# Five score banks, one pool of four weight tiles and block transposes for every duo in a decoder layer on one core

## The chip, the core and the metric

The kernel runs on one core of one Trainium2 chip. A core has five engines that run side by side, each through its own list of instructions in order: TensorE (PE, matrix products; PEld is its loading of the stationary operand), VectorE (DVE), ScalarE (ACT), GpSimd (POOL) and SyncE (SP, which here only issues transfers). SBUF is the working memory of 128 partitions. PSUM receives the products; it has 8 banks, and a bank holds 512 float32 values in each partition. Transfers (DMAs) are issued from an engine's queue and carried out by 16 transfer engines. An instruction starts when the semaphores that it waits for have reached their values.

The metric is the device time of one execution in microseconds (us). The time before is 1978.22 us, the median of 3 runs (1977.18 to 1980.28).

## The reference

It is one decoder layer in float32 on x of shape 4 x 1024 x 256: self-attention, cross-attention to 64 context rows, and a feed-forward part that picks one of 64 small networks for each row. Each part is added to its input.

```python
x = x + attn(layernorm(x))     # 16 heads of 64, 4 key/value heads, all 1024 keys, no mask
x = x + xattn(layernorm(x))    # 16 heads of 16, 64 keys
x = x + ffn(layernorm(x))      # gelu and tanh to two numbers, choice of 1 of 64 splines, layernorm

# attn, for each batch, head and query row
scores = einsum('bqhd,bkhd->bhqk', q * scale, k)
probs = softmax(scores)
out = einsum('bhqk,bkhd->bqhd', probs, v)
```

Nearly all of the work is the self-attention: 4 batches x 16 heads x 1024 x 1024 scores.

## The kernel before

**Tiles.** A batch has 8 query tiles of 128 rows. A query tile has 8 head pairs (two heads z = 0, 1 that lie in the two halves of the partitions), so that there are 4 x 8 x 8 = 256 "rows" of work: one row is 128 queries of two heads against 1024 keys. Two rows (i = 0, 1) make a duo; there are 128 duos, 32 in each batch.

**One row** (function `duo`, lines 566 to 688). `scores` (L592) multiplies queries with keys: 4 products of 512 keys, two for each head, into a PSUM tile `s` of two banks per head. `largest` (L606, VectorE) takes the maximum of each head's 1024 scores. `exponential` (L612, ScalarE) writes the softmax weights, before division, into the tile `prob` and adds up their sum.

**The weights' transpose.** For the product with the values the weights must lie with the keys on the partitions. There are two ways to that. For three duos of four (`by_array(d)` false) VectorE transposes 32 x 32 blocks in place (`turn`, L621, one instruction of 128 x 1024 per head and row), and 16 transfers from SyncE's queue (`carry`, L648, 128 KB each) move the blocks from `prob` to their partitions in a second tile, `probT`. For the fourth (d % 4 == 3) TensorE transposes 128 x 128 tiles (`flips`, L631) into PSUM tiles of the pool `p1`, and ScalarE copies them out (L635).

**The product with the values** (`values`, L671) reads `probT` in two parts into a PSUM tile `av` with a bank of its own, and ScalarE copies it to `heads` (L686). `project` (L691) inverts the sums, spreads them over the partitions through DRAM (`rsT`, `rsD`, `rb`), divides on GpSimd (L710), and multiplies with the output weights (L728).

**Beside the rows** run the projections of queries, keys and values (L545, L494, L517), the layer norms (L403), the cross-attention (from L797) and the feed-forward part (from L1023), as tasks that fill the time between.

**PSUM.** `s` has 2 tiles of 2 banks, `p1` 3 banks, `av` 1: all 8. `prob` and `probT` have 2 places each.

**The order of work** is not that of the loops. Every step is handed to a planner, the class `Flow` (L78 to L189), by `add(engine, cost, key, emit, reads, writes, ...)`: its engine, an assumed cost in us, a due number, what it reads and writes. `order` then plays through time and always takes the task that can start first, score, maximum and exponential ("urgent") before others, and in this order the instructions are written into the engines' lists. A task's results count as ready for other engines after a lag (`LAG`, or a `lag` of its own for transfers). `places` says how many tiles of each name there are. `SLACK` keeps a task from being put just ahead of an urgent one that is about to be ready. What really runs waits on semaphores; a wrong cost only makes a poorer order.

Of the kernel before, what the change touches and what calls it, by code (L numbers as in the profile page):

```python
# [17 lines left out]
P = 128  # L18
# [38 lines left out]
class Buf:  # L57


    def __init__(self, tag=None, make=None, whole=None):  # L60
        self.tag, self.make, self.whole = tag, make, whole or self
        self.writers, self.readers, self.parts = [], [], {}
        self.uses, self.first, self.left, self.last, self.t = set(), None, 0, 0.0, None

# [13 lines left out]
class Flow:  # L78
# [7 lines left out]
    AHEAD, SLACK = 16, 0.4  # L86
    LAG = {"PE": 0.3, "DVE": 0.2, "ACT": 0.25, "POOL": 0.25}
# [5 lines left out]
    def add(self, engine, cost, key, emit, reads=(), writes=(), lag=None, holds=(), lead=False, urgent=False):  # L93
# [4 lines left out]
        for b in writes:  # L98
            t.need.update(b.readers)
        t.need.discard(t)  # L100
# [19 lines left out]
    def order(self):  # L120
        free = {tag: [0.0] * n for tag, n in self.places.items()}
# [14 lines left out]
        while todo:  # L136
            best = None
            for engine, some in could.items():
                pick = None
                soon = min((t.ready for t in some if t.urgent), default=inf)  # L140
                for t in some:
# [4 lines left out]
                    for b in t.takes:  # L146
# [4 lines left out]
                        start = max(start, free[b.tag][k])  # L151
                    else:
                        if not t.urgent and start < soon < start + t.cost - self.SLACK:
                            start = soon
# [10 lines left out]
            for b in t.takes:  # L165
                free[b.tag].pop(0)
                if b.tag in self.lines:
                    self.lines[b.tag].remove(b)
# [8 lines left out]
            for b in t.bufs:  # L177
                b.left -= 1
                b.last = max(b.last, t.end)
                if not b.left:  # L180
                    insort(free[b.tag], b.last + 0.2)
            yield t

    def emit(self):
        for t in self.order():
            for b in t.takes:
                b.t = b.make()
# [5 lines left out]
def decoder(  # L193
# [26 lines left out]
    ps_s = ctx.enter_context(tc.tile_pool(name="ps_s", bufs=2, space=PSUM))  # L220
    ps_1 = ctx.enter_context(tc.tile_pool(name="ps_1", bufs=3, space=PSUM))
    ps_o = ctx.enter_context(tc.tile_pool(name="ps_o", bufs=1, space=PSUM))
# [5 lines left out]
            s=2, p1=3, o=1, x=3, xn1=2, xT=1, kT0=1, kT1=1, vn=4, qT=12, prob=2, probT=2, sums=3, nmax=4,  # L228
# [8 lines left out]
    def buf(tag, pool, *shape, bufs=None, name=None):  # L237
        bufs = flow.places[tag] if bufs is None else bufs
        return Buf(tag, lambda: pool.tile([P, *shape], F32, tag=tag, name=name or tag, bufs=bufs))

    def psum1(name):

        return Buf("p1", lambda: ps_1.tile([P, 512], F32, tag="p1", name=name))
# [159 lines left out]
    def layernorm(key, name, src, dst, w, reads, writes):  # L403

        st = Buf("ln", lambda: (
            small.tile([P, w, 6], F32, tag="bnst", name=f"{name}_st", bufs=2),
            small.tile([P, w, 2], F32, tag="bnmv", name=f"{name}_mv", bufs=2),
            small.tile([P, w], F32, tag="bnrs", name=f"{name}_rs", bufs=2),
# [20 lines left out]
        add("DVE", 0.6 * w, key, stats, reads, [st], holds=writes)  # L429
        add("POOL", 1.0, key, rsqrt, [st], [st])  # L430
        add("ACT", 0.45 * w, key, apply, [st, *reads], writes)

    def transposed(key, name, src, dst, k, reads, write):
# [12 lines left out]
        add("PE", 0.55, key, flips, reads, [pt], holds=[write])  # L446
# [6 lines left out]
    halves = (slice(0, HD), slice(HD, P))  # L453
    xs, xTs, kTs, vns, qTs, sums, heads = {}, {}, {}, {}, {}, {}, {}

    def by_array(d):

        return d % 4 == 3
# [27 lines left out]
    def keys(b, j, key):  # L486

        kT = kTs[b, j] = buf(f"kT{j}", big, S, name=f"kT_{b}_{j}")
        for g in range(2):
# [15 lines left out]
            add("PE", 1.75, key, project, [wk_, xTs[b].part(2 * g), xTs[b].part(2 * g + 1)], [pk], holds=[kT])  # L505
            add("ACT", 0.7, key, evict, [pk, colv_], [kT])

    def value_rows(b, g, key):
# [24 lines left out]
        add("PE", 1.75, key, project, [wv_, xTs[b].part(g)], [pv], holds=[vn])  # L533
        add("DVE", 0.69, key, evict, [pv, rowv_], [vn])

    def queries(b, w, c, key):
# [16 lines left out]
        add("PE", 1.8, key, project, [wq_, xTs[b].part(w)], [pq], holds=[qTs[b, w, c], qTs[b, w, c + 1]])  # L553
# [12 lines left out]
    def duo(b, d):  # L566
# [7 lines left out]
        prob = Buf("prob", lambda: work.tile([P, 4 * S], F32, tag="prob", name=f"prob_{b}_{d}"))  # L574
        probT = Buf("probT", lambda: work.tile([P, 4 * S], F32, tag="probT", name=f"probT_{b}_{d}"))
# [7 lines left out]
        for i in range(2):  # L583
# [3 lines left out]
            ps = [Buf("s", lambda z=z: ps_s.tile([P, S], F32, tag="s", name=f"s_{b}_{d}_{i}_{z}")) for z in range(2)]  # L587

            def scores(ps=ps, q=q, kT=kT):
                for g in range(2):  # L590
                    for z, r in enumerate(halves):
                        mm(  # L592
                            ps[z].t[:, 512 * g : 512 * (g + 1)],
# [6 lines left out]
            add("PE", 1.95, n - 3, scores, [q, kT], ps, holds=[prob, ss], lead=True)  # L600
            for z in range(2):
                k = z * QC + c
                nmax = buf("nmax", small, 1, name=f"nmax_{b}_{d}_{i}_{z}")

                def largest(z=z, nmax=nmax, ps=ps):
                    nc.vector.tensor_reduce(nmax.t, ps[z].t, AX.X, ALU.max, negate=True)  # L606

                def exponential(z=z, i=i, k=k, nmax=nmax, ps=ps):
                    src = ps[z].t
# [6 lines left out]
                add("DVE", 1.22, n - 3, largest, [ps[z]], [nmax], urgent=True)  # L616
                add("ACT", 1.33, n - 3, exponential, [ps[z], nmax], [prob.part((z, i)), ss.part(k)], urgent=True)
                if not by_array(d):
# [4 lines left out]
                    add("DVE", 1.25, n - 1, turn, [prob.part((z, i))], [prob.part((z, i))])  # L623
                else:
                    for g in range(2):
# [11 lines left out]
                        add("PE", 0.54, n - 1, flips, [prob.part((z, i))], [pt], holds=[probT])  # L637
                        add("ACT", 0.6, n - 1, evict, [pt], [probT.part((z, g))])

        if not by_array(d):  # L640


            for k in range(4):
                for qb in range(4):
                    r = (qb + k) % 4

                    def carry(qb=qb, r=r):
                        nc.sync.dma_start(  # L648
# [654 lines left out]
```

## Time and profile before

| what | value |
|---|---|
| median of 3 runs | 1978.22 us |
| the profiled execution: its time | 1978.13 us |
| its span, first to last instruction | 1976.4 us |
| TensorE busy | 1737.7 us (88%) |
| VectorE busy | 1400.9 us (71%) |
| ScalarE busy | 1062.5 us (54%) |
| GpSimd busy | 554.1 us (28%) |
| mean granted TensorE clock | 0.939 of full speed |
| block transfers | 1536, all from SyncE's queue |

In the lines of the profile, "L606 DVE TENSOR_REDUCE nmax<-s 128x1 f32<-128x1024 f32 x512 | 601.9, 1216 | 342.7 <-PE s L592 341.4" reads: line 606, VectorE, the operation, output and input with shapes, 512 of them, 601.9 us busy in all, 1216 ns for one; the engine was idle for 342.7 us just before them, of which 341.4 ended when TensorE's scores of line 592 were done. Two instructions that follow each other closely overlap at their ends, so that the busy time of a group is less than its count times the duration of one. A float32 product is two instructions on TensorE. Semaphore and transfer-issuing instructions do not count as busy. In a timeline the columns are start, length, engine, line and operation, and in brackets the idle time before.

### The profile page before, as it was taken

The numbers are of one execution on the slowest core, as the hardware profiler recorded it, in microseconds if no ns is written. First come the engines' busy times: TensorE is split into PE (matmuls) and PEld (weight loads), VectorE is DVE, ScalarE is ACT, GpSimd is POOL, SyncE is SP. The second block draws the span as 40 slices with busy tenths as digits, with TensorE's granted clock in tenths as the row PEclk, the third lists the DMA queues.
The fourth block names the chain that finished last, engine by engine and source line by source line (L and its number), as shares of the span: only waits on it lengthen the run. The fifth ranks groups of instructions, "written<-read, shape, count | busy, mean of one in ns | idle before, by whom it ended". The sixth has DMA issues, their size and how long they took to land.

```text
span 1976.4 us, 28894 instructions
## 1 busy us (share of the span) xinstructions
PE 1737.7 (88%) x10180; PEld 1025.7 (52%) x10180; DVE 1400.9 (71%) x2036; ACT 1062.5 (54%) x1977; POOL 554.1 (28%) x872
## 2 busy tenths in 40 slices
PE   6898989889998998989999898988999899997842
PEld 4455555555654555555655454555555455554521
DVE  4667777886778766787677676787677876778632
ACT  3445556656564655655565555655565455555511
POOL 1001213152122512225031522316122350304352
PEclk8889999999998999999999898999999899999965
DMA  3566455455655455566454456545555645445500
GB/s 131 128 139 150 115 140 122 115 146 125 138 129 136 106 137 124 121 152 150 102 134 107 123 136 139 139 116 126 136 116 116 157 118 129 105 111 130 139 23 12
DMA packets 95455, 243.05 MB, mean 123 GB/s; under 512 B 28368, under 2 KB 39376, under 8 KB 95312
## 3 DMA queue, kind: packets, MB, share of 16 engines
q1 hardware_dynamic: 91504, 229.39, 49.6%
q0 software_dynamic: 2704, 9.46, 1.7%
q10 hardware_dynamic: 1104, 2.37, 0.3%
q8 instruction: 81, 1.33, 0.3%
q14 instruction: 62, 0.51, 0.1%
HBM read 35.32 MB, written 4.46 MB: 20 GB/s over the span
## 4 chain that ended last, share of the span: by engine, by line
PE 64%; DVE 16%; ACT 6%; POOL 5%; DMA 3%; SPq 3%; issue 3%; POOLq 0%; DVEq 0%; ACTq 0%
PE s L592 22%; PE av L671 18%; DVE nmax L606 6%; PE pq L545 5%; PE po L728 4%; PE ptp L631 4%; DVE prob L621 3%; SPq L648 3%; ACT prob L612 3%; PE pk L494 1%; PE pv L517 1%; DMA par<-in_table,tile 1%; PE pxt L898 1%; PE xs L837 1%; PE pxq L814 1%
## 5 line engine op out<-in xcount | busy, mean ns | idle before, releaser
L606 DVE TENSOR_REDUCE nmax<-s 128x1 f32<-128x1024 f32 x512 | 601.9, 1216 | 342.7 <-PE s L592 341.4
L612 ACT ACTIVATE prob<-s,nmax 128x1024 f32<-128x1024 f32 x512 | 568.8, 1114 | 407.3 <-DVE nmax L606 388.7
L592 PE MATMUL s<-kT,qT 64*128 64x512 f32 x2048 | 584.4, 639 | 35.0 <-ACT prob L612 34.6
L671 PE MATMUL av<-probT,vn 128*64 128x256 f32 x4096 | 499.4, 396 | 29.5 <-DMA probT<-prob 26.0
L621 DVE STREAM_TRANSPOSE prob<-prob 128x1024 f32<-128x1024 f32 x384 | 458.6, 1223 | 37.7 <-ACT prob L612 26.8
L671 PEld LDWEIGHTS av<-probT,vn 128*64 128x64 f32 x4096 | 298.2, 142 | 252.3 <-issue 111.7
L592 PEld LDWEIGHTS s<-kT,qT 64*128 64x128 f32 x2048 | 212.9, 192 | 266.5 <-issue 163.6
L710 POOL TENSOR_TENSOR heads<-heads,rb 128x256 f32<-128x256 f32 x128 | 90.0, 729 | 607.6 <-DMA rb<-rsD 503.7
L635 ACT COPY probT<-ptp 128x512 f32<-128x512 f32 x256 | 137.8, 590 | 74.3 <-PE ptp L631 72.5
L631 PE MATMUL ptp<-ident,prob 128*128 128x128 f32 x1024 | 141.1, 281 | 34.0 <-ACT prob L612 30.4
L631 PEld LDWEIGHTS ptp<-ident,prob 128*128 128x128 f32 x1024 | 112.8, 143 | 82.4 <-issue 37.6
L545 PE MATMUL pq<-ln_T,wq 128*128 128x256 f32 x512 | 127.6, 394 | 12.3 <-DVE xsc L849 12.3
L863 POOL TENSOR_TENSOR xsc<-xsc,xmx 128x1024 f32<-128x1024 f32 x32 | 61.2, 1914 | 248.2 <-DVE xmx L860 136.7
L728 PE MATMUL po<-wo,heads 128*128 128x256 f32 x512 | 119.2, 383 | 1.6 <-POOL heads L710 1.6
L545 PEld LDWEIGHTS pq<-ln_T,wq 128*128 128x128 f32 x512 | 95.3, 194 | 47.9 <-issue 29.2
L728 PEld LDWEIGHTS po<-wo,heads 128*128 128x128 f32 x512 | 95.5, 190 | 29.8 <-POOL heads L710 9.2
L612 ACT ACTIVATION_READ_ACCUMULATOR prob<-s,nmax 128x1 f32 x512 | 101.0, 197 | 0.0
L427 ACT ACTIVATE ln_n<-x,ln_mv,ln_rs 128x256 f32<-128x256 f32 x64 | 36.6, 596 | 107.1 <-POOL ln_mv L422 107.1
L686 ACT COPY heads<-av 128x256 f32<-128x256 f32 x128 | 47.6, 372 | 76.3 <-PE av L671 73.9
L556 ACT ACTIVATE qT<-pq,bqs,qscale 128x256 f32<-128x256 f32 x128 | 65.6, 564 | 35.6 <-PE pq L545 35.5
L419 POOL TENSOR_SCALAR ln_rs<-ln_mv 128x1 f32<-128x1 f32 (+1 forms) x96 | 21.4, 222 | 213.2 <-DVE ln_mv L415 200.7
L441 PE MATMUL ln_pt<-ident,ln_n 128*128 128x128 f32 x192 | 37.2, 312 | 44.9 <-ACT ln_n L427 42.4
(166 smaller groups left out, 1498.1 us busy)
## 6 DMA issues: line engine op xcount, KB each, us to landing
probT<-prob SPq DMA_DIRECT2D x1536, 128.0 KB, 2.3
rb<-rsD SPq DMA_DIRECT2D x64, 256.0 KB, 3.9
ln_n<-in_x SPq DMA_DIRECT2D x16, 256.0 KB, 3.1
x<-in_x SPq DMA_DIRECT2D x8, 512.0 KB, 4.9
out<-ln_n POOLq DMA_DIRECT2D x7, 512.0 KB, 4.9
wq<-in_w_qT ACTq DMA_DIRECT2D x1, 1024.0 KB, 8.0
wo<-in_w_oT SPq DMA_DIRECT2D x1, 1024.0 KB, 12.6
rowv<-in_rows ACTq DMA_DIRECT2D x1, 774.0 KB, 10.6
```

The costliest lines, as they stand in the source:

```text
L545: mm(pq.t[:, 2 * P * k : 2 * P * (k + 1)], lhsT=wq[:, dc, (c + k) * P : (c + k + 1) * P], rhs=xTs[b].t[:, dc, 2 * P * w : 2 * P * (w + 1)] ...
L556: nc.scalar.activation(qTs[b, w, c + k].t, pq.t[:, 2 * P * k : 2 * P * (k + 1)], AF.Identity, bias=bqs[:, c + k : c + k + 1], scale=qscale,)
L592: mm(ps[z].t[:, 512 * g : 512 * (g + 1)], lhsT=q.t[r, (qt % 2) * P : (qt % 2 + 1) * P], rhs=kT.t[r, 512 * g : 512 * (g + 1)], start=True, ...
L606: nc.vector.tensor_reduce(nmax.t, ps[z].t, AX.X, ALU.max, negate=True)
L612: nc.scalar.activation(weights(prob.t, z, i), src, AF.Exp, bias=nmax.t, accum_out=ss.t[:, k : k + 1])
L621: nc.vector.transpose(t, t)
L631: flip(pt.t[:, j * P : (j + 1) * P], weights(prob.t, z, i)[:, kc * P : (kc + 1) * P], ident)
L635: nc.scalar.copy(to[:, z, 4 * g : 4 * g + 4, i, :], pt.t.rearrange("p (c q) -> p c q", q=P))
L671: mm(av.t[r, :], lhsT=vns[b, kc // 2].t[:, kc % 2, j * HD : (j + 1) * HD], rhs=rhs, start=(kc == 0), stop=(kc == NT - 1),)
L710: nc.gpsimd.tensor_tensor(hT[e].t, hT[e].t, rb.t[:, 2 * e : 2 * e + 2, :], ALU.mult)
L728: mm(po.t[:, :D], lhsT=hT[c // 2].t[:, c % 2], rhs=wo[:, c, :], start=(c == 0), stop=(c == QC - 1))
L863: nc.gpsimd.tensor_tensor(sc.t, sc.t, mx.t.unsqueeze(2).to_broadcast([P, XH, SK]), ALU.subtract)
```

## The change

- `by_array` always answers no: all 128 duos go by VectorE's block transposes and 16 transfers each, 2048 transfers in all. Of each duo's 16 the last four in the loop (k == 3) are issued from ScalarE's queue, the other twelve from SyncE's.
- The scores get one PSUM tile of five banks in place of two tiles of two. The rows rotate over the banks in three ways, and the scores are handed to the planner as two halves, each of which writes one bank per head and waits for the last reader of just these banks (`over`).
- `prob` and `probT` share one pool of four places instead of two and two.
- The product `av` takes a tile of the pool `p1`; its own bank has gone to the scores.
- The planner names the place that each tile takes (`place`, tags such as `prob_2`), drops `SLACK`, has smaller lags and other costs. The tiles of other steps change in name only.

```diff
-    AHEAD, SLACK = 16, 0.4
-    LAG = {"PE": 0.3, "DVE": 0.2, "ACT": 0.25, "POOL": 0.25}
+    AHEAD = 16
+    LAG = {"PE": 0.15, "DVE": 0.1, "ACT": 0.1, "POOL": 0.15}
...
+        for b in over:
+            t.need.update(b.readers)
+            b.readers, b.writers = [], [t]
...
-                        if not t.urgent and start < soon < start + t.cost - self.SLACK:
-                            start = soon
...
-                free[b.tag].pop(0)
+                b.place = free[b.tag].pop(0)[1]
...
-                    insort(free[b.tag], b.last + 0.2)
+                    insort(free[b.tag], (b.last + 0.1, b.place))
...
-            s=2, p1=3, o=1, x=3, xn1=2, xT=1, kT0=1, kT1=1, vn=4, qT=12, prob=2, probT=2, sums=3, nmax=4,
+            p1=3, x=3, xn1=2, xT=1, kT0=1, kT1=1, vn=4, qT=12, prob=4, sums=3, nmax=4,
...
+    score_banks = ps_s.tile([P, 5, 512], F32, name="score_banks")
+    banks = [Buf() for _ in range(5)]
...
     def by_array(d):
 
-        return d % 4 == 3
+        return False
...
-        prob = Buf("prob", lambda: work.tile([P, 4 * S], F32, tag="prob", name=f"prob_{b}_{d}"))
-        probT = Buf("probT", lambda: work.tile([P, 4 * S], F32, tag="probT", name=f"probT_{b}_{d}"))
+        prob = Buf("prob", lambda k: work.tile([P, 4 * S], F32, tag=f"prob_{k}", name=f"prob_{b}_{d}", bufs=1))
+        probT = Buf("prob", lambda k: work.tile([P, 4 * S], F32, tag=f"prob_{k}", name=f"probT_{b}_{d}", bufs=1))
...
-            def scores(ps=ps, q=q, kT=kT):
-                for g in range(2):
+            ways = (((0, 0), (2, 0)), ((3, 1), (0, 0)), ((1, 1), (3, 0)))[int(n) % 3]
+            ps = [score_banks[:, way[0] : way[0] + 2, :].rearrange("p g k -> p (g k)") for way in ways]
+            for part in range(2):
+                to = [way[0] + (part ^ way[1]) for way in ways]
+
+                def scores(part=part, ways=ways, to=to, q=q, kT=kT):
                     for z, r in enumerate(halves):
+                        g = part ^ ways[z][1]
                         mm(
-                            ps[z].t[:, 512 * g : 512 * (g + 1)],
+                            score_banks[:, to[z], :],
...
-            add("PE", 1.95, n - 3, scores, [q, kT], ps, holds=[prob, ss], lead=True)
+                add(
+                    "PE", 0.97, n - 3, scores, [q, kT], over=[banks[k] for k in to], holds=[prob, ss], lead=True
+                )
...
-                add("DVE", 1.22, n - 3, largest, [ps[z]], [nmax], urgent=True)
-                add("ACT", 1.33, n - 3, exponential, [ps[z], nmax], [prob.part((z, i)), ss.part(k)], urgent=True)
+                add("DVE", 1.17, n - 3, largest, mine, [nmax], urgent=True)
+                add("ACT", 1.14, n - 3, exponential, [*mine, nmax], [prob.part((z, i)), ss.part(k)], urgent=True)
...
-                    def carry(qb=qb, r=r):
-                        nc.sync.dma_start(
+                    engine, queue, cost = ("ACT", nc.scalar, 0.45) if k == 3 else ("SP", nc.sync, 0.68)
+
+                    def carry(qb=qb, r=r, queue=queue):
+                        queue.dma_start(
...
-        av = Buf("o", lambda: ps_o.tile([P, 2 * P], F32, tag="o", name=f"av_{b}_{d}"))
+        av = psum1(f"av_{b}_{d}")
```

## The prediction

> **What bounds the kernel now.** I read the page's busy shares first, then the costliest groups, then who waited for whom, then one row in the timeline, then the transfers.
>
> ```profile
> PE 1737.7 (88%) x10180; PEld 1025.7 (52%) x10180; DVE 1400.9 (71%) x2036; ACT 1062.5 (54%) x1977; POOL 554.1 (28%) x872
> ...
> L606 DVE TENSOR_REDUCE nmax<-s 128x1 f32<-128x1024 f32 x512 | 601.9, 1216 | 342.7 <-PE s L592 341.4
> L612 ACT ACTIVATE prob<-s,nmax 128x1024 f32<-128x1024 f32 x512 | 568.8, 1114 | 407.3 <-DVE nmax L606 388.7
> L592 PE MATMUL s<-kT,qT 64*128 64x512 f32 x2048 | 584.4, 639 | 35.0 <-ACT prob L612 34.6
> L671 PE MATMUL av<-probT,vn 128*64 128x256 f32 x4096 | 499.4, 396 | 29.5 <-DMA probT<-prob 26.0
> L621 DVE STREAM_TRANSPOSE prob<-prob 128x1024 f32<-128x1024 f32 x384 | 458.6, 1223 | 37.7 <-ACT prob L612 26.8
> ...
> L635 ACT COPY probT<-ptp 128x512 f32<-128x512 f32 x256 | 137.8, 590 | 74.3 <-PE ptp L631 72.5
> L631 PE MATMUL ptp<-ident,prob 128*128 128x128 f32 x1024 | 141.1, 281 | 34.0 <-ACT prob L612 30.4
> ```
>
> TensorE is busy 88% of the span. VectorE and ScalarE idle mostly in a ring: maximum waits for scores (341 us), exponential for maximum (389 us). The next view gives busy time by stage: the 256 rows of scores run from 39 to about 1871 us, and 106 us of tail follow.
>
> ```profile
> 39.00:1881.00 1842.00, 1686.50 (x9996) 993.90 (x9995) 1361.30 (x1879) 1033.10 (x1926) 506.98 (x767) 0.96 0.55 128
> 39.00:146.00 107.00, 96.60 (x482) 55.84 (x483) 70.72 (x70) 51.18 (x95) 3.50 (x5) 0.89 0.54 123
> 450.00:500.00 50.00, 50.00 (x311) 29.43 (x309) 32.59 (x37) 28.94 (x55) 8.57 (x15) 1.00 0.56 128
> ```
>
> The columns after the length are PE, PEld, DVE, ACT, POOL, granted clock, DMA share and GB/s. The first maximum starts at 38.9 and the last at 1869.2, so a row takes (1869.2 + 1.2 - 38.9) / 256 = 7.15 us. Divided by 256, the first line gives each engine's load per row: PE 6.59, DVE 5.32, ACT 4.04 us. So TensorE is the bound, with 0.56 us a row to spare; at 450 to 500 us it has none. The timeline shows the ring of one row:
>
> ```profile
> 803.29 1.99 PE L592 MATMUL s<-kT,qT 64*128 64x512 f32 x8
> 805.31 2.36 DVE L606 TENSOR_REDUCE nmax<-s 128x1 f32<-128x1024 f32 x2 [2.11 <-PE s L592]
> 806.57 1.11 ACT L612 ACTIVATE prob<-s,nmax 128x1024 f32<-128x1024 f32 x1 [0.22 <-DVE nmax L606]
> 807.70 1.11 ACT L612 ACTIVATE prob<-s,nmax 128x1024 f32<-128x1024 f32 x1
> 807.82 3.11 PE L592 MATMUL s<-kT,qT 64*128 64x512 f32 x8 [0.29 <-ACT prob L612]
> 810.79 2.31 DVE L606 TENSOR_REDUCE nmax<-s 128x1 f32<-128x1024 f32 x2
> 810.89 10.05 SPq L648 DMA_DIRECT2D probT<-prob  x16
> ```
>
> Maximum to maximum the ring takes 810.79 - 805.31 = 5.48 us. The second scores start after the first exponential, stop inside for the second, and take 3.11 us where 1.99 would do: stall that the page books as busy. The last line is one duo's 16 block transfers, 10.05 us of issues.
>
> **The change, part by part** (per row, 256 rows, two rows to a duo).
>
> Array transposes of 32 duos go. TensorE loses 141.1 us of busy time: 0.55 a row. ScalarE loses the 137.8 us of copies: 0.54 a row.
>
> Block transposes instead: 32 duos x 4 = 128 more on VectorE. One costs 458.6 / 384 = 1.194 us of busy time, so 152.9 us: 0.60 a row. Nothing covers them if VectorE becomes the fullest engine; today its 29% idle would.
>
> Five banks and scores in two halves. The first half needs the first exponential of the row before, the second half the second one, with other matmuls allowed between. The ring shortens: from the maximum's start to the second exponential's end is 808.81 - 805.31 = 3.50 us, then one half of scores, 1.0 us, and about 0.2 us of signals (0.22 idle stands before the exponential above): 4.7 instead of 5.48. In-score stall: 584.4 / 256 = 2.28 a row against 1.99 dense, so 0.29 at most is won and 0 at least, since the wait may only move into idle time; I take 0.15.
>
> ScalarE issues 4 of a duo's 16 transfers, 512 in all. None is in the trace there. SP's issue of this very shape took 589 ns (median); ScalarE's loads at the start took 0.45. So 0.9 to 1.2 us a row; I take 1.2, the same transfer. ScalarE: 4.04 - 0.54 + 1.2 = 4.7. What is queued behind such an issue is the next exponential, and behind that the next scores. SP still issues 1536, its quarter fewer per duo making up for a third more duos. In the built program 4 issues a duo on ScalarE stand among the next duo's exponentials. The first one waits for the last duo's transfers to land.
>
> Semaphore waits: the built program has 225 more semaphore instructions on VectorE and 315 more on ScalarE, as one tile pool makes each reuse wait for eight transfer semaphores. In the trace's records such instructions follow each other at 97 ns on VectorE and 77 ns on ScalarE: 0.09 and 0.09 a row. TensorE has 291 more; between nothing (they pass while matmuls run) and 0.26 us each, the mean of the 636 waits of 163.6 us put down to issue ahead of score weights, so 0 to 0.3 a row. I take 0, since most weight loads run ahead of matmuls that are still busy; the 0.3 goes into the upper end.
>
> Four weight tiles in one pool. A duo's transposed tile can take the place of the tile just sent, so a duo's transfers wait for those of the duo before. Transfer time: queue q1 had 49.6% of 1976.4 us for 229.39 MB, 980 us, so a transfer of 128 KiB is 0.56 us of all 16 engines and a duo's 16 are 9.0; with the other 120 us of q1 and the 2.4% on other queues (47 us; together 1.3 us a duo) that is 10.3 of a duo's 13.5. By issues, 12 on SP at 0.64 and the 2.3 us to landing make 10.0. Both are under two rows, so beside other work. Cover gone: at rows under 5.2 us transfers would bind.
>
> ```profile
> q1 hardware_dynamic: 91504, 229.39, 49.6%
> ...
> probT<-prob SPq DMA_DIRECT2D x1536, 128.0 KB, 2.3
> ```
>
> The Trainium skill, DMA: Bandwidth & Descriptors, "Issuing engines are not separate DMA queues", says that DMAs of all issuers run interleaved on the same 16 engines, which speaks against the move to a second queue. By it a duo's transfers fall from 10.05 us to the 9.0 of engine time, not to SP's 12 x 0.64 = 7.7; the sum stays, since both are hidden.
>
> The value product moves from its own bank into the pool of three, which loses 256 array-transpose tiles and gains 128 longer ones. It costs 0 as long as a bank is free. If not, a projection starts late: bound by the 0.42 to 0.6 us of an eviction per duo, 0 to 0.3 a row.
>
> The planner's new costs and lags only reorder; I give them nothing, between a gain of the whole spare 0.56 and a loss of the same.
>
> Tail: the last duo was an array duo, whose last exponential ended at 1871.5 and whose product ended around 1881. Now a transpose (1.2), 7.7 of issues, 2.3 landing and 3.7 of product stand there: 14.9 instead of 9.3, so +6 us.
>
> **The sum.** TensorE 6.59 - 0.55 - 0.15 = 5.89. VectorE 5.32 + 0.60 + 0.09 = 6.01: it is the fullest, TensorE 2% behind. Before, the row stood 0.56 above the fullest engine; from 39 to 146 us, 16 rows at 6.69 stood 0.65 above its 96.60 / 16 = 6.04. With two engines nearly level I take 0.75. Row 6.76, 256 rows 1730; 39 before, 106 + 6 after: 1881 of span, 1883 with the 1.7 that the profiled run (1978.13) has around its span. That run stands 0.1 us under the median of 1978.22, so nothing is corrected.
>
> A rule against it: the Trainium skill, Perfetto Trace Analysis, "Identifying the Most-Contended Engine", calls matmul busy time a bad measure and asks for weight-load time. That is 52% here, so by it TensorE is not full, taking matmuls away gives nothing, and the sum would be 1978 + 6 = 1984. The window from 450 to 500 us, with 50.00 of 50 busy at the full clock, speaks for the busy time as read here.
>
> **Rivals.**
> 1. The ScalarE queue stops (slower). Place: the first block transfer of each duo on ScalarE, which waits for the landing of the previous duo's. For it: a landing took up to 7.2 us, and engines at some 75% queue up. Against: 10.0 to 10.3 us against 13.5 leaves 3 us. It decides from (7.15 - 6.76) x 2 = 0.8 us of lost exponential time a duo; at 2 us a duo, 128 x 2 = 256 on 1883 gives 2139, at 1.2 us 2037. I take 2037.
> 2. VectorE, in order and full, serves maxima late behind transposes: 1.0 above its load, row 7.0, 1945. For: a third more transposes of 1.2 us now stand between the maxima. Against: the ring is 0.8 shorter.
> 3. The shorter ring tells fully: 0.35 above load, row 6.36, 1781. For: 342 us of VectorE's idle is that ring. Against: nothing in the trace has run that close to a load for long but 450 to 500 us.
> 4. TensorE was not the limit; the banks only move the wait: 1978.
>
> **How the numbers follow.** Forecast (1825 to 1930) 0.50; rival 1 0.21; rival 2 0.12; rival 3 0.13; rival 4 0.04. The likeliest is 1883. Below 1795 I leave 0.07 (row 6.4) and above 2010 about 0.12, the worse half of rival 1. What separates a change from none here is 0.2%, 4 us: faster 0.50 + 0.12 + 0.13 = 0.75, same 0.04, slower 0.21.
>
> **What would show it.** Right: VectorE's share near 1560 / 1881 = 83%, above or level with TensorE's; no L631; the maximum's idle before it on scores well under 341; score matmuls near 2.0 us per eight; spacing of maxima 6.8 a row. Wrong: ScalarE's exponential or transfer issue waiting for transfers by more than 100 us (rival 1); VectorE over 88% (the surplus overestimated); the product waiting for transfers by far more than 26 us, which would mean that the transfers, not VectorE, set the row.

## The result and the profile after

The changed kernel takes 2233.28 us (median of 4 runs) against 1979.25 us before: a ratio of 1.1276, 95% interval 1.1243 to 1.131. It is 12.8% slower where the forecast had 1883 us, and the time lies outside the range of 1795 to 2010. The profiled execution has a span of 2231.3 us.

The page of the kernel after, busy times and transfer queues:

```profile
span 2231.3 us, 28421 instructions
...
PE 1686.0 (76%) x9156; PEld 906.0 (41%) x9156; DVE 1553.5 (70%) x2164; ACT 928.9 (42%) x1721; POOL 556.4 (25%) x872
...
q1 hardware_dynamic: 91504, 229.39, 42.7%
q10 hardware_dynamic: 25680, 69.52, 13.0%
```

VectorE is busy 153 us longer than before, as costed. TensorE is busy only 52 us less, though the 141.1 us of array transposes are gone: its other matmuls take longer. No engine is full any more. q1 carries SyncE's transfers and q10 ScalarE's. The time is in waiting, and the costliest groups of the kernel after, with up to three releasers of each (what ended its waits), say where:

```profile
L630 DVE STREAM_TRANSPOSE prob<-prob 128x1024 f32<-128x1024 f32 x512 | 613.9, 1224 | 226.5 <-ACT prob L621 219.0 <-DMA probT<-prob 2.7 <-issue 2.4
L615 DVE TENSOR_REDUCE nmax<-score_banks 128x1 f32<-128x1024 f32 x512 | 602.2, 1218 | 304.2 <-PE score_banks L597 299.1 <-issue 2.6 <-ACT ln_n L425 2.3
L597 PE MATMUL score_banks<-kT,qT 64*128 64x512 f32 x2048 | 601.2, 702 | 391.4 <-ACT prob L621 391.2
L621 ACT ACTIVATE prob<-score_banks,nmax 128x1024 f32<-128x1024 f32 x512 | 567.2, 1111 | 819.8 <-DVE nmax L615 618.9 <-DMA probT<-prob 40.9 <-DVE cl_cf L974 30.0
L682 PE MATMUL av<-probT,vn 128*64 128x256 f32 x4096 | 512.3, 401 | 4.5 <-DMA probT<-prob 3.8 <-ACT xoT L936 0.5 <-issue 0.2
```

TensorE now waits 391 us ahead of the scores for exponentials; before it was 35. The exponentials wait 619 us for maxima; before it was 389. Both are steps of the ring maximum, exponential, scores. The product waits only 3.8 us for transfers, and the exponentials 40.9. By stage, with the same columns as before (PE, PEld, DVE, ACT, POOL, granted clock, DMA share, GB/s):

```profile
39.00:2110.00 2071.00, 1618.58 (x8869) 862.84 (x8869) 1499.62 (x1966) 890.88 (x1654) 507.04 (x762) 0.91 0.60 144
450.00:500.00 50.00, 36.00 (x175) 19.51 (x174) 37.01 (x62) 16.23 (x30) 12.78 (x21) 0.76 0.53 126
```

The first maximum starts at 37.9 us and the last ends at 2111.0, so a row takes (2111.0 - 37.9) / 256 = 8.10 us instead of 7.15. Between 450 and 500 us, where TensorE was full before, it now works 36 of 50 us at a clock of 0.76. The timeline of one row shows the new ring:

```profile
1004.99 2.35 DVE L615 TENSOR_REDUCE nmax<-score_banks 128x1 f32<-128x1024 f32 x2 [0.32 <-PE score_banks L597]
...
1007.38 1.11 ACT L621 ACTIVATE prob<-score_banks,nmax 128x1024 f32<-128x1024 f32 x1 [1.94 <-DVE nmax L615]
...
1008.48 1.11 ACT L621 ACTIVATE prob<-score_banks,nmax 128x1024 f32<-128x1024 f32 x1
...
1009.73 3.61 PE L597 MATMUL score_banks<-kT,qT 64*128 64x512 f32 x8 [4.58 <-ACT prob L621]
...
1013.46 2.36 DVE L615 TENSOR_REDUCE nmax<-score_banks 128x1 f32<-128x1024 f32 x2 [3.31 <-PE score_banks L597]
```

Before, the first exponential started 806.57 - 805.31 = 1.26 us after the first maximum, so when its own maximum was there, and the scores started 2.51 us after it, behind the first exponential. Now the first exponential starts at 2.39 us, behind both maxima (1004.99 + 2.35 = 1007.34), and the scores at 4.74 us, behind both exponentials (1008.48 + 1.11 = 1009.59). Maxima, exponentials and scores no longer overlap: the ring takes 8.47 us here instead of 5.48. The scores take 3.61 us in this row, where the granted clock is at half speed; the median row takes 1.99 in both kernels, but the mean is 2.73 instead of 2.28. The wait for both maxima is in every row: from the first maximum's start to the second exponential's end the median is 4.66 us after and 3.50 before.

Why each step waits for both heads stands in the built program. Counting for each instruction whose result its semaphore wait asks for, over 256 rows:

```
                                         before   after
first exponential waits for
  its own (first) maximum                  256        0
  the second head's maximum                  0      256
```

The trace agrees: the first exponential starts behind the second maximum in all 256 rows after, and in 13 before. Of the first halves of the scores, which by the planner need the first exponential of the row before, 218 of 255 ask for the second one.

The scheduler in the kernel text tracks five banks one by one, but the five banks are one PSUM tile. The layer below, which sets the semaphores, orders these accesses as if to one place: here a reader of two banks is made to wait for another engine's earlier read of two others. So VectorE's second maximum comes before ScalarE's first exponential, and the scores mostly wait for both exponentials, though no byte is shared.

### The profile page after: what moved, and what is told of

It reads as the page before. It is cut to its first block, busy times and chain, and to the rows that moved or that the text cites. A ratio compares the mean times of both kernels' runs of the same rounds, so it can differ in the third digit from the quotient of the medians.

```text
span 2231.3 us, 28421 instructions
## 1 busy us (share of the span) xinstructions
PE 1686.0 (76%) x9156; PEld 906.0 (41%) x9156; DVE 1553.5 (70%) x2164; ACT 928.9 (42%) x1721; POOL 556.4 (25%) x872
## 4 chain that ended last, share of the span: by engine, by line
PE 36%; DVE 22%; ACT 15%; DMA 10%; issue 7%; SPq 5%; ACTq 4%; POOL 2%; DVEq 0%; POOLq 0%
PE score_banks L597 21%; DVE nmax L615 15%; ACT prob L621 13%; DMA probT<-prob 9%; PE av L682 6%; SPq L659 4%; ACTq L659 4%; DVE prob L630 3%; PE pq L545 2%; PE po L739 1%; PE pxq L825 1%; PE ln_pt L439 1%; PE pv L517 1%; PE xs L848 1%; DMA xwo<-in_xw_o 1%
## 5 line engine op out<-in xcount | busy, mean ns | idle before, releaser
L621 ACT ACTIVATE prob<-score_banks,nmax 128x1024 f32<-128x1024 f32 x512 | 567.2, 1111 | 819.8 <-DVE nmax L615 618.9
L597 PE MATMUL score_banks<-kT,qT 64*128 64x512 f32 x2048 | 601.2, 702 | 391.4 <-ACT prob L621 391.2
L615 DVE TENSOR_REDUCE nmax<-score_banks 128x1 f32<-128x1024 f32 x512 | 602.2, 1218 | 304.2 <-PE score_banks L597 299.1
L630 DVE STREAM_TRANSPOSE prob<-prob 128x1024 f32<-128x1024 f32 x512 | 613.9, 1224 | 226.5 <-ACT prob L621 219.0
L597 PEld LDWEIGHTS score_banks<-kT,qT 64*128 64x128 f32 x2048 | 190.6, 205 | 628.1 <-ACT prob L621 485.3
L621 ACT ACTIVATION_READ_ACCUMULATOR prob<-score_banks,nmax 128x1 f32 x512 | 100.5, 196 | 0.0
L896 POOL TENSOR_TENSOR xsc<-xsc,xrs 128x1024 f32<-128x1024 f32 x32 | 60.8, 1901 | 37.3 <-DVE xrs L893 37.2
L745 POOL TENSOR_TENSOR x<-x,res 128x256 f32<-128x256 f32 x32 | 23.3, 728 | 181.8 <-DVE res L742 178.7
L949 POOL TENSOR_TENSOR x<-x,xres 128x256 f32<-128x256 f32 x32 | 23.2, 726 | 178.3 <-DVE xres L946 178.3
L825 PE MATMUL pxq<-ln_T,xwq 128*128 128x256 f32 x128 | 52.6, 581 | 16.6 <-ACT ln_T L442 16.6
```

Source lines behind the costliest of these rows:

```text
L597: mm(score_banks[:, to[z], :], lhsT=q.t[r, (qt % 2) * P : (qt % 2 + 1) * P], rhs=kT.t[r, 512 * g : 512 * (g + 1)], start=True, stop=True,)
L615: nc.vector.tensor_reduce(nmax.t, ps[z], AX.X, ALU.max, negate=True)
L621: nc.scalar.activation(weights(prob.t, z, i), src, AF.Exp, bias=nmax.t, accum_out=ss.t[:, k : k + 1])
L630: nc.vector.transpose(t, t)
L825: mm(pq.t[:, n * c : n * (c + 1)], lhsT=xwq[:, dc, c * P : (c + 1) * P], rhs=xT.t[:, dc, :], start=(dc == 0), stop=(dc == DC - 1),)
```

## The experiments

Theory A: the one PSUM tile acts as one lock, and that lengthens the ring. Rivals (theories B and C): the block transfers or their places, VectorE's extra transposes, ScalarE's issues.

**e1: the lock alone, in the kernel before.**

```diff
+    score_banks = ps_s.tile([P, 4, 512], F32, name="score_banks")
-            ps = [Buf("s", lambda z=z: ps_s.tile([P, S], F32, tag="s", name=f"s_{b}_{d}_{i}_{z}")) for z in range(2)]
+            ps = [Buf("s", lambda z=z: score_banks[:, 2 * z : 2 * z + 2, :].rearrange("p g k -> p (g k)")) for z in range(2)]
```

> The kernel before with one edit: the two score tiles of two banks become two halves of one PSUM tile of four banks, at fixed places. Order of work, transposes, transfers, pools, number of banks in use: all as before. Theory A (one tile is one lock): in the built program the first head's exponential then waits for the second head's maximum, and the first scores of the next row for the second exponential. The ring of a row, 5.48 us before, becomes maxima 2.36 + exponentials 2.24 + scores 2.0 + about 0.3 of signals = 6.9 us; with 1.2 to 1.4 us more in each of 256 rows the kernel takes 2150 to 2330 us. Theory B (the loss comes from the ScalarE queue or from the transfers): nothing of that is in this kernel, 1975 to 1985 us.

Measured: 2127.99 us, 1.0739 (1.0705 to 1.0772) of before. The arithmetic, the order and the banks are those of before; only the two tiles have become one. Its timeline shows the same ring:

```profile
802.11 2.36 DVE L610 TENSOR_REDUCE nmax<-score_banks 128x1 f32<-128x1024 f32 x2 [0.45 <-PE score_banks L596]
...
804.56 1.11 ACT L616 ACTIVATE prob<-score_banks,nmax 128x1024 f32<-128x1024 f32 x1 [4.54 <-DVE nmax L610]
...
805.67 1.10 ACT L616 ACTIVATE prob<-score_banks,nmax 128x1024 f32<-128x1024 f32 x1
...
806.91 3.79 PE L596 MATMUL score_banks<-kT,qT 64*128 64x512 f32 x8 [4.85 <-ACT prob L616]
```

In its built program all 256 first exponentials wait for the other head's maximum, and in its trace all 256 start behind it. The lock costs 146 us by itself, a little less than the 2150 us and more that theory A expected.

**e2: the changed kernel without the lock.** The scores get the PSUM layout of before (two tiles of two banks, the product in a bank of its own, scores in one step); all the rest of the change stays.

```diff
-    score_banks = ps_s.tile([P, 5, 512], F32, name="score_banks")
...
+            ps = [
+                Buf("s", lambda k, z=z: ps_s.tile([P, S], F32, tag=f"s_{k}", name=f"s_{b}_{d}_{i}_{z}", bufs=1))
+                for z in range(2)
+            ]
...
-        av = psum1(f"av_{b}_{d}")
+        av = Buf("o", lambda k: ps_o.tile([P, 2 * P], F32, tag="o", name=f"av_{b}_{d}", bufs=1))
```

> The changed kernel with the PSUM layout of before: two score tiles of two banks, scores as one task, the value product in a bank of its own. All duos by block transposes, one pool of four weight tiles, a quarter of the transfers on ScalarE's queue, the planner's new costs: kept. Theory A (one tile is one lock): the false waits are gone, the ring is 5.48 us again, and the loads of the prediction (VectorE 6.0, TensorE 5.9 us a row) set a row of 6.8 to 7.1 us: 1880 to 1970 us. Theory B (ScalarE's queue or transfers waiting for transfers): stays above 2150 us, with SyncE's queue waiting for transfers by some 500 us as in the changed kernel.

Measured: 1975.7 us, 0.9978 (0.9963 to 0.9993). That takes 258 us off the changed kernel. It also takes away the halves of the scores and the product's place in the pool of three; a five-bank layout without the lock was not tried, so what these two do by themselves stays open. The same exchange of layouts is worth 0.120 of the time before between e4 and e5 below, 0.156 between e3 and e6, and 0.079 between e12 and e9. But e2 is only 0.2% faster than before, not the 4.8% of the forecast: there is a second error.

**e3 and e4: two parts undone with the lock in place.**

```diff
-                    engine, queue, cost = ("ACT", nc.scalar, 0.45) if k == 3 else ("SP", nc.sync, 0.68)
+                    engine, queue, cost = ("SP", nc.sync, 0.68)          # e3
-        return False
+        return d % 4 == 3                                                 # e4
```

> The changed kernel with all 16 transfers of a duo issued from SyncE's queue. Theory A: the ring through the one score tile still sets the row; 2200 to 2270 us, ScalarE's exponentials still waiting for maxima by some 600 us. Theory B (the exponentials stand behind transfer issues on ScalarE): falls below 2100 us.

> The changed kernel with every fourth duo by array transposes again. Theory A: the ring sets the row, not VectorE's load or the transfers; 2190 to 2280 us though VectorE loses 153 us of work. Theory C (VectorE's 128 more transposes or the transfers are the bound): falls below 2100 us.

Measured: e3 1.1473 (1.1446 to 1.15), e4 1.101 (1.0971 to 1.105), against 1.1276 after. All transfers on SyncE is a little worse under the lock, array transposes for every fourth duo a little better. Both lie just outside what theory A expected (2273.6 us against 2200 to 2270, 2179.7 against 2190 to 2280), on opposite sides. Neither comes near the time before, so neither part is the main cause.

**e5 to e8: what holds e2 at the time before.** All four start from e2. e5 brings the array duos back, e6 puts all transfers on SyncE (edits as above), e7 leaves out the block transposes in every fourth duo (`if d % 4 != 3` ahead of `turn`'s `add`), e8 has three score tiles:

```diff
-            s=2, p1=3, o=1, x=3, xn1=2, xT=1, kT0=1, kT1=1, vn=4, qT=12, prob=4, sums=3, nmax=4,
+            s=3, p1=2, x=3, xn1=2, xT=1, kT0=1, kT1=1, vn=4, qT=12, prob=4, sums=3, nmax=4,
...
-        av = Buf("o", lambda k: ps_o.tile([P, 2 * P], F32, tag="o", name=f"av_{b}_{d}", bufs=1))
+        av = psum1(f"av_{b}_{d}")
```

> The changed kernel with the PSUM layout of before and every fourth duo by array transposes again: what is left of the change is the pool of four weight tiles, ScalarE's share of the transfers in the other duos, and the planner's costs. Theory V (with two score tiles the block transposes of the last quarter of duos eat the gain on VectorE): faster than the two-tile kernel's 1976, 1900 to 1950 us. Theory T (the transfers eat it): the same range, since a quarter of them goes too. Theory P (what is left of the change gains nothing, and neither do the transposes): 1970 to 1990 us.

> The two-tile kernel with all 16 transfers of a duo on SyncE's queue. Theory T (transfer time per duo sets the row): 16 issues of 0.64 us instead of 12 make a duo's transfers later by up to 1.5 us, so 2000 to 2170 us. Theory V (VectorE is the limit, transfers lie beside): 1960 to 1985 us, or a little less as ScalarE loses 512 issues.

> The two-tile kernel without VectorE's block transposes in every fourth duo (these duos' weights are then wrong); their 16 transfers stay. VectorE loses 128 x 1.19 = 153 us. Theory V: the row follows VectorE's load, 0.3 to 0.6 us a row less, 1820 to 1900 us. Theory T: the transfers still set the row, 1955 to 1985 us. Theory P (TensorE, whose busy time is hardly less than before, 1714 us, as its matmuls got longer): 1940 to 1980 us.

> The two-tile kernel with three score tiles of two banks and two banks for everything else, the value product among it. The scores of a row can then start after the first exponential of the row before, not after the second, without a shared tile. Theory R (the ring through scores, maxima and exponentials still costs the two-tile kernel its time): the ring falls from 5.48 to about 4.6 us and the kernel to 1880 to 1950 us, if two banks are enough for the rest. Theory V or T (VectorE or transfers): 1960 to 2000 us, more if products wait for a bank.

Measured: e5 0.9811 (0.9783 to 0.9838), e6 0.9912 (0.9885 to 0.994), e7 0.9935 (0.9909 to 0.9961), e8 0.9839 (0.9814 to 0.9864). e7 takes 136 us of busy time off VectorE (1542.3 to 1406.5) and wins 0.4%: VectorE isn't the bound, though the forecast made it the fullest engine. The quarter on ScalarE costs 0.7%; that 16 issues from one queue would make the transfers later and the kernel slower, 2000 us and more, did not come. A fourth of the duos without transfers (and without their block transposes, the 0.4% of e7) wins 1.7%, though it gives TensorE 1024 transposes back. The third score tile wins 1.4%, within what was expected if the ring still costs e2 time.

**e9 to e12: separate places.** Two places each for `prob` and `probT` instead of the pool of four, in e2, in e8 and in the changed kernel (e9, e10, e12); e11 is e10 with the array duos back and all transfers on SyncE.

```diff
-            s=2, p1=3, o=1, x=3, xn1=2, xT=1, kT0=1, kT1=1, vn=4, qT=12, prob=4, sums=3, nmax=4,
+            s=2, p1=3, o=1, x=3, xn1=2, xT=1, kT0=1, kT1=1, vn=4, qT=12, prob=2, probT=2, sums=3, nmax=4,
...
-        probT = Buf("prob", lambda k: work.tile([P, 4 * S], F32, tag=f"prob_{k}", name=f"probT_{b}_{d}", bufs=1))
+        probT = Buf("probT", lambda k: work.tile([P, 4 * S], F32, tag=f"probT_{k}", name=f"probT_{b}_{d}", bufs=1))
```

> The two-tile kernel (1976) with two places for the weights and two for the transposed weights, as before, in place of the pool of four. Theory S (in the pool of four a duo's transfers wait until those of the duo before have landed: 10.5 us of issues and some 3 us of gap make 14 us a duo, which is the two-tile kernel's duo): the transfers of neighbouring duos overlap again, 1880 to 1940 us. Theory D (the 16 transfer engines themselves are full): 1960 to 1985 us. Theory V (VectorE): 1960 to 1985 us.

> The three-tile kernel (1947) with two places for the weights and two for the transposed weights. Theory S: its transfers were in series even more (88% of its duos begin their transfers later than their last transpose), so it gains at least as much, 1820 to 1900 us. Theory D or V: 1930 to 1960 us.

> Three score tiles, own pools, every fourth duo by array transposes as before, all transfers on SyncE's queue, the planner's new costs. Theory S with the fewest transfers and the shorter ring: TensorE is the bound again with 6.6 us a row and some 0.4 above it, 1850 to 1920 us. If two banks are too few for the array transposes beside the value product: 1930 to 2000 us.

> The changed kernel with two places for the weights and two for the transposed weights, the one tile of five score banks kept. Theory A (the one score tile sets the row of 8.1 us): 2170 to 2230 us, the transfers being off its path except for the 37% of duos that wait for them. Theory S alone (the serial transfers account for the whole loss): below 2050 us.

Measured: e9 1.0627 (1.0607 to 1.0646), e10 1.0096 (1.0064 to 1.0128), e11 1.0136 (1.009 to 1.0182), e12 1.1413 (1.1392 to 1.1435). The theory behind these runs (S), that the shared pool holds the transfers up, fell: without the pool e2 loses 6.5% (1.0627 / 0.9978), and all four runs lie above every range that was expected of them. The list of waits of e9 shows what the pool prevents; in e2 the same line has 34.8 us:

```profile
ACT prob L616 <- DMA probT<-prob: 108.4, 30, 9.1
```

With two places, an exponential that begins a new duo waits until the transfers out of the tile two duos back have landed.

**e13 and e14: the transfers.** Theory T now: with the lock gone, the transfers of neighbouring duos in series set the row. Rival O: the planner's order does.

```diff
-        probT = Buf("prob", lambda k: work.tile([P, 4 * S], F32, tag=f"prob_{k}", name=f"probT_{b}_{d}", bufs=1))
+        probT = prob
...
-                        queue.dma_start(
-                            out=probT.t[32 * r : 32 * r + 32, S * qb : S * (qb + 1)],
-                            in_=prob.t[32 * qb : 32 * qb + 32, S * r : S * (r + 1)],
-                        )
```

That is e13: all of `carry` goes, and the product reads `prob`. In e14 `carry` stays, with half the size, and the product reads the first head's half for both heads:

```diff
-                            out=probT.t[32 * r : 32 * r + 32, S * qb : S * (qb + 1)],
-                            in_=prob.t[32 * qb : 32 * qb + 32, S * r : S * (r + 1)],
+                            out=probT.t[32 * r : 32 * r + 32, S * qb : S * qb + S // 2],
+                            in_=prob.t[32 * qb : 32 * qb + 32, S * r : S * r + S // 2],
```

> Two score tiles as in e2, and the block transfers left out altogether: the value product reads the weights tile that VectorE turned, so that its operand is the wrong block order (the output leaves out the move of blocks between partitions). All 128 duos keep their block transposes, the pool keeps four places. Theory T (with the one-tile lock gone, the transfers of neighbouring duos in series set the row: 10.48 us of issues and some 3 us to the next duo's first one make the 14.28 us per duo of e2): the row falls to what TensorE has to do; its 1713.9 us of busy time in e2 hold some 72 us of stall in the scores (656 against 584 before), so about 1640 plus the spare 8% that before had, 1780 to 1900 us. Rival O (the planner's new order and the semaphore waits cost what is missing, the transfers run beside): 1950 to 1985, as e2's 1975.7.

> e2 with each of the 16 transfers of a duo cut to its first half (64 KB, the head z = 0), and the product using these weights for both heads (the second head's weights are left out of the move). The number of issues, their queues, waits and places stay. If what sets the row is the time of the 16 transfer engines or the landing (theory T by bytes), about half of what e13 gains: 1860 to 1945. If it is the issue of 16 transfers from the queues (T by issues) or not the transfers at all (rival O): 1960 to 1985.

Measured: e13 1899.57 us, 0.9602 (0.9572 to 0.9631), at the upper end of what T expected; e14 1926.04 us, 0.9737 (0.9702 to 0.9771). So the transfers cost e2 0.9978 - 0.9602 = 3.8% of the time before, about 75 us, and half the bytes with the same 16 issues bring 2.4% back, some 48 us of these. (e13 also frees the places that `probT` takes in the pool; e14 does not.) Rival O falls as the account of these 75 us. SyncE's waits for transfers, first of e2 and then of e14:

```profile
SPq L654 <- DMA probT<-prob: 407.0, 343, 4.2
```

```profile
SPq L654 <- DMA probT<-prob: 222.4, 195, 5.2
```

In e2 one duo's issues span 10.48 us in the mean, and from the last of them to the first of the next duo it is 3.80 (the median is 2.99), so that a duo takes 14.28 us, and two rows take as long. 49% of the duos start their transfers more than 0.3 us after their last block transpose, 149 us in all, so they stand ready and wait; in e14 it is 19% and 37 us. In the kernel before, which moved three duos of four, it was 8%. This lateness is no price by itself: e6 has 70% and 357 us, e8 88% and 465 us, and both are faster than e2.

**e15 and e16: whether the gains add up.** e15 is e8 with the array duos back, e16 is e5 with all transfers on SyncE.

> Three score tiles of two banks, product in the pool of two, and every fourth duo by array transposes, with the pool of four and ScalarE's quarter. By theory T, array duos (no transfers) and a third score tile (slack ahead of the scores) both give the rows room: if what each gains adds up, 1947 - 39 = 1908, 1895 to 1920. If both cure the same wait, or the array transposes' 256 tiles starve the pool of two: 1930 to 1960.

> Two score tiles, every fourth duo by array transposes (as e5, 1936.8), and all transfers from SyncE's queue. In e2 against e6 the quarter on ScalarE cost 16 us with 128 transfer duos; with 96 it should cost three quarters, 12 us: 1920 to 1930. Rival: SyncE's 16 issues of a duo with the array duo between have slack, and ScalarE's quarter costs nothing: 1932 to 1942.

Measured: e15 1.0132 (1.0106 to 1.0157), e16 0.9755 (0.9726 to 0.9783). e16 is the fastest whole kernel found, 1929.89 us, and takes 2.5% less time than the one before. Its step from e5 has about the size expected. In e15 the gains don't add up, they more than cancel, and its 2004.7 us lie above both ranges expected: three score tiles alone give a row of 6.97 us (e8), array duos alone 6.94 (e5), both 7.21, and e11, which also has both, 7.20. That the pool of two is too small for the array transposes' tiles and the product fits this, but was not isolated.

**e17 and e18: what the change is worth in e16.** e17 has two places each (edit as in e9), e18 the planner's lags and SLACK rule of before.

> e16 with two places each for prob and probT in place of the pool of four. What e16 keeps of the change is the pool of four and the planner's costs, lags and missing SLACK; together they gave 0.9755 of the time before. If the pool is what gains there (places for the exponentials while transfers land): 1965 to 1990 here. If the planner's numbers gain: 1925 to 1940.

> e16 with the planner's lags (0.2 to 0.3 us) and the SLACK rule of before; the costs stay as the change has them. If the pool of four is what gains in e16: 1925 to 1940, as e16. If the lags and the dropped rule gain: 1960 to 1985.

Measured: e17 0.9851 (0.9827 to 0.9875), e18 0.9852 (0.9823 to 0.9881). Each theory expected the whole gain on its side; it is 1.0% for the pool of four and 1.0% for the lags with the dropped rule, and both times lie between the ranges.

## Why the prediction was wrong

The span after is 2231.3 us against the forecast's 1881. The rows explain it: 256 x (8.10 - 6.76) = 343 us, and the tail 8 us (120.3 after the last maximum instead of 112). Rows of the runs between split the 343 us: after to e2 256 x (8.10 - 7.11) = 253, e2 to e13 256 x (7.11 - 6.81) = 77, and 13 are left. The first part is the PSUM layout, with e1 showing the lock worth 146 in the kernel before; why it costs more here was not separated. The second is the transfers, which the forecast took as hidden.

**"Five banks and scores in two halves" is the step that failed.** It took a ring of 4.7 us: 3.50 from the first maximum to the second exponential's end, one half of scores, 0.2 of signals. The 3.50 stands for a first exponential that runs beside the second maximum. In the built program it can't: the stretch is 1009.59 - 1004.99 = 4.60 us in the row shown after and 806.77 - 802.11 = 4.66 in e1, one maximum more, and a whole step of scores follows it, 2.0 us at full clock, so 6.9 instead of 4.7. The step trusted what the planner was told (`over` with single banks) and never asked what the semaphores wait for. The forecast had counted 225 and 315 more semaphore instructions there and costed their issue, 0.09 us a row, but not what they wait for.

**The clock had no term.** Granted half-speed time is 244.5 us before, 363 in e1, 476 after. Of the score matmuls 5.0% took over 800 ns before, 14.2% in e1 and 18.2% after. How much of the loss this is was not tested; e4, with the lock and the array duos, takes 2180 us with only 261 us at half speed.

**"Four weight tiles in one pool" was right that the transfers fit under two rows and wrong that this hides them.** It compared 10.0 to 10.3 us with 13.5. Measured in e2 are 10.48 of issues and 3 to 4 to the next duo's first issue, which fill the two rows, and SyncE waits 407 us for landings in between. e13 prices the transfers at 77 us, 0.30 a row, where the forecast had nothing unless rows fell under 5.2 us. That the next `probT` waits for the place of a tile that has not landed fits this, but was not isolated. The pool itself is a gain, not a cost (e9, e17).

**"ScalarE issues 4 of 16"** had the right price: 512 issues at 607 ns (median) are 1.21 us a row, and 890.88 / 256 + 1.21 = 4.69 against 4.7. But it saves little: the mean span of a duo's issues is 11.11 us with one queue (e6) and 10.48 with two (e2), where the four issues moved, at some 0.6 us each, would make 2.4. The Trainium skill, DMA: Bandwidth & Descriptors, "Issuing engines are not separate DMA queues", says that DMAs of all issuers run on the same 16 engines. The 0.6 us saved instead of 2.4 agrees with it. In time e6, with one queue, is 0.7% faster than e2.

**"Array transposes go"** held for ScalarE, whose busy time fell by 133.6 us against 137.8, but not for TensorE: 141.1 us went, and its busy time fell by 51.7. **"Block transposes instead"** held as a load: the block transposes grew from 458.6 to 613.9, 155 us against 152.9. But the sum made VectorE the fullest engine at 6.01 us a row; it is 1499.62 / 256 = 5.86, and e7 shows that it doesn't bind.

**The sum was nearly right where nothing locks or moves, for the wrong reason.** e13, with no transfers, has rows of 6.81 us against 6.76:

```profile
39.00:1782.00 1743.00, 1616.97 (x8904) 887.98 (x8904) 1482.72 (x1966) 898.63 (x1657) 506.86 (x762) 0.94 0.07 19
```

TensorE's load there is 1616.97 / 256 = 6.32 us, not 5.89, and the row stands 0.49 above it, not 0.75 above VectorE. The group of scores in e13 holds the difference:

```profile
L596 PE MATMUL s<-kT,qT 64*128 64x512 f32 x2048 | 650.4, 664 | 102.3 <-ACT prob L616 101.9
```

650.4 / 256 = 2.54 us a row where the forecast took 2.28 - 0.15 = 2.13: 0.41 of the missing 0.43. Of the 0.55 a row that the array transposes freed on TensorE, 0.26 came back as longer scores (584.4 to 650.4 us), and the 0.15 that the forecast took off the scores was not won. How much of this is stall and how much half clock was not separated. Longer scores speak against taking busy time as a fixed load. They agree in part with the warning of the Trainium skill, Perfetto Trace Analysis, "Identifying the Most-Contended Engine", that matmul busy time is "not a good measure of how close you are to roofline".

**"The planner's new costs and lags ... I give them nothing"** was off by about 1%: lags and rule gain that much in e16 (e18).

**The rivals.** The slower one, the ScalarE queue, priced 0.21, was the right sign by the wrong mechanism: the exponentials wait only 40.9 us for transfers. Rival 4, that the banks only move the wait, is the nearest, but it had no loss in it. Of the signs given as wrong, none came in the changed kernel (VectorE 70%, the exponentials' wait for transfers 40.9 us, the product's 3.8), so they did not tell of this loss. Those listed as right that failed most plainly are VectorE's share, 70% and not 83%, and the spacing of the maxima, 8.1 us and not 6.8; eight score matmuls take 2.0 us in the median row, but 2.73 in the mean.

## What to carry to other kernels

Before a shorter ring is priced, read in the built program what each instruction of the ring waits for: sub-tiles that a kernel's own planner keeps apart may be one tile to the layer that sets the semaphores, and then they share one order. Give each independently reused PSUM buffer a tile of its own. That transfers take less time than the rows beside them doesn't hide them: here they took 10.5 us of 14.3 and cost 0.3 us a row. Where the next transfers need the place of the last ones, count the time to landing too.

## What the runs showed of the hardware

The granted clock is recorded with two values only, full and half. In the kernel after, the score matmuls of the row at 1009.73 us, at half clock, took 881 to 1216 ns each, those of the row at 1003.06, at full clock, 589. Half-speed time does not follow the row's length: it is 181 us in e16 (row 6.96), 244.5 before (7.15), 363 in e1 (7.75) and 476 after (8.10), but 362 in e2 (7.11) and 261 in e4 (7.92). Without the lock, the runs with array duos have 181 to 250 us and those without 294 to 453. What sets it was not tested.

Halving a duo's bytes shortened the span of its issues only from 10.48 to 9.52 us, but SyncE's waits for landed transfers from 407 to 222 us: this reads as the bytes setting mainly when transfers land, not how fast they are issued.
